# Two-layer transformer: four self-attention norms turned by TensorE instead of by DMAs, and the feed-forward norm of batch 0 earlier and in quarters

## The chip, the core and the metric

The kernel runs on one core of a Trainium2 chip. The metric is the device time of one execution in microseconds; several runs are taken and the median is given.

The engines, by the names of the profile: PE is TensorE (matmuls; PEld is its weight load, which overlaps), DVE is VectorE, ACT is ScalarE, POOL is GpSimd, SP is SyncE. SP does no arithmetic in this kernel: it is one in-order queue that issues nearly all DMAs after the start.

## The reference, cut to what matters

```
def _ln(x, g, b):
    m = mean(x); v = mean(square(x - m))
    return (x - m) * rsqrt(v + EPS) * g + b

def layer(x, context):                       # twice, with weights of its own
    h1 = _ln(x, n1_g, n1_b)
    x = _attn(h1, h1, q1, k1, v1, o1_w, o1_b, heads) + x
    h2 = _ln(x, n2_g, n2_b)
    x = _attn(h2, context, q2, k2, v2, o2_w, o2_b, heads) + x
    h3 = _ln(x, n3_g, n3_b)
    a, g = split(h3 @ ff_w1 + ff_b1, 2)
    return a * gelu(g) @ ff_w2 + ff_b2 + x
```

`_attn` is softmax attention with 20 heads of width 16. x is 4 batches x 512 tokens x 320, the context 4 x 1601 x 192, the hidden width of the feed-forward part 1280. All is 32-bit float. Each of the two layers has three norms per batch: 2 x 3 x 4 = 24 norms in the program.

## The kernel before, in words

**Units.** The order of all work is written out by a Python program that runs when the kernel is built. It goes through a list of units. An attention unit is one layer, self or cross, one batch b and one group g of four heads (5 groups). Self attention has 4 chunks of 128 keys per unit, cross attention 13. A feed-forward unit is one batch. Per layer come 20 self units, 20 cross units, 4 feed-forward units, so unit 37 is layer 0's cross attention, batch 3, group 2. The builder counts half chunks (`clock["round"]`): 8 per self unit, 26 per cross unit.

**A chunk** (`main`, L1270) issues for its unit the scores (L1280, matmul `st`, with the row maxima `nrows` as a third product), exponentials on ACT (L1290), and the products with the values (L1306, eight records per chunk, `av`), copied by ACT (L1325) and summed by POOL (L1326). In the same chunk it issues for the *next* unit the products of which only the row maxima are wanted: PE L1054 (`sps`), DVE L1069 (reductions to `nmax` or `pm`). At the end of a unit the maxima are laid out as rows (L1107 to L1131) and carried by DMA to `nrows`. The values' product comes once per chunk at a fixed place, so the distance between two of them is a chunk's length.

**Side work.** Everything else (norms, projections of queries, keys and values, the output's projection, the context's transposes) lies in queues, `chains`, entered by `add` (L428) with a cost in PE time, a due half chunk and two conditions. `steps` (L473) is called once or twice a chunk; it picks the due-first head whose conditions hold, and pays with a credit that `pace` fills. Steps with the cost LIGHT need no PE: at most `lights` of them are taken per call, which is 2 in a chunk without other products, 1 otherwise. At its end `steps` calls `carry` (L784), which puts DMAs on SP's queue: first the moves of finished queries and keys (L852), then errands, then the norms' bands, at most three per call.

**Side work by its names in the trace.** Projection of self attention's queries and keys: PE L886 (`qkps`), whose banks ACT empties into high and low halves (L897, L902, buffers `high` and `low`), which the moves (L852) carry to `q` and `kT`. Cross attention's queries: L927 (`qps`). Values: L1015 (`vps`). The context of a batch is turned into `ctxT`, stored by L741 and read back as the operand `w` by L755 (eight DMAs in two groups of four).

**A norm** (`add_norm`, L537) does for its batch, in this order:

- statistics of four token tiles of 128 tokens (DVE, L546 and L547), then the reciprocal root (L507 to L523: started on DVE, two Newton steps on POOL);
- then one of two forms, since the product needs features on partitions:
  - **the turned form** (`first` is true): three DVE scalings per token tile write the normalised tile in a permuted order to a buffer named `hturned` (`plain`, L608); TensorE turns it, four transposes per part and three parts (`turn`, L621, into a bank `hps`); ACT empties each part with gain and bias (L629) straight into `hT`;
  - **the DMA form**: per token tile one DVE normalisation to `hn` (L562) and one DVE transpose of 32 x 32 blocks into `hturned` (L568); then DMAs put the blocks into place in `hT` (`spread` and `move`, L578: 12 for a self or cross norm, 16 for a feed-forward norm); POOL applies gain and bias, three instructions (`affine`, L595);
- at last the next bias is added to x on POOL (`biased`, L601).

`due` is a norm's last date; its steps are due some fixed half chunks before. In the DMA form they are due `EARLIER` = 14 half chunks sooner than in the turned form, except feed-forward norms. `together` says how many token tiles one LIGHT step takes: two for a feed-forward norm, one otherwise. `landed` says how many half chunks `affine` waits after the last DMA of a part was issued: 4, and 2 for a feed-forward norm (`LANDS`). There is one `hturned` buffer; of `hT` there are two.

Before the change the turned form is used by self attention's norms of batches 0 and 1 in layer 0, and by cross attention's norm of batch 0 in both layers. The 20 others have the DMA form.

`add_norms` (L1372) enters the norms a few units ahead. A feed-forward norm gets `due` = its unit's start - 4.

Of the kernel before, what the change touches and what calls it, by code (L numbers as in the profile page):

```python
# [75 lines left out]
def kernel(ctx: ExitStack, tc: tile.TileContext, x, context, ws, out):  # L76
# [306 lines left out]
    clock = {"round": 0, "credit": 0.0, "lights": 0, "tiles": None, "ff": False}  # L383
# [142 lines left out]
    EARLIER = 14  # L526


    LANDS = (4, 2)
# [7 lines left out]
    def add_norm(l, b, i, put, done, due):  # L537
        xb = xs[b]
        s = {}
# [93 lines left out]
                hn_used.remove(b)  # L633
                put(s["hT"])

        first = i == 0 and b < 2 and l == 0 or i == 1 and b == 0
        ahead = 0 if first or i == 2 else EARLIER
        parts = [(0, 0, P, 0), (1, 4, 96, 0), (2, 7, 96, 0)]
        if i == 2:
            parts = [(0, 0, P, 0), (1, 4, P, 0), (2, 8, REST, 0), (2, 8, REST, REST)]  # L640
        left, moved = [len(parts) * P // SLOT], {}
# [2 lines left out]
            return lambda: clock["round"] >= s[key] + n  # L644

        def together(f):
            return [lambda ts=ts: [f(t) for t in ts] for ts in (((0, 1), (2, 3)) if i == 2 else ((0,), (1,), (2,), (3,)))]

        for t, f in enumerate(together(stats)):
            add(  # L650
                "norm", LIGHT, f, due - ahead - 22 + t,
                (lambda: stage[b] == 3 * l + i and not hn_used and b in loaded) if t == 0 else yes,
                (lambda: b == 0 or clock["round"] >= loaded[b] + 5) if t == 0 else yes,
            )
# [14 lines left out]
        for t, f in enumerate(together(lambda t: (normalise(t), blocks(t)))):  # L669
            add("norm", LIGHT, f, due - ahead - 13 + t, yes, yes if t else later(1))  # L670
# [3 lines left out]
            return lambda: k in moved and (k < 2 or not left[0])  # L674

        def landed(k):
            return lambda: clock["round"] >= moved[k] + LANDS[i == 2] and clock["round"] > s.get("scaled", 0)

        for k, n in enumerate((P, P, P) if i == 2 else (P, 96, 96)):
            add("scale", 0.0, lambda k=k, n=n: affine(k, n), due - 6 + k, there(k), landed(k))  # L680
# [87 lines left out]
    def lead(u):  # L768

        if u.i == 0:  # L770
            return 0
        return units[u.i - (AHEAD - 1 if u.early else 2 if u.m == 0 else 1)].start
# [595 lines left out]
    ff_read = []  # L1368
# [3 lines left out]
    def add_norms(i):  # L1372

        while norms and norms[0].i <= i + ((1 if norms[0].b else 3) if norms[0].kind == "ff" else AHEAD + 1 if norms[0].early else 8):
            u = norms.popleft()
            if u.kind == "ff":
                add_norm(u.l, u.b, 2, lambda t, u=u: setattr(u, "hT", t), lambda u=u: u in ff_read, u.start - 4)
            else:

                def done(u=u):  # L1380
                    return u.made["q"] == G and (u.cross or u.made["k"] == G and u.vmade[1] == u.nch)

                due = lead(u) - (10 if u.cross else 28)
                add_norm(u.l, u.b, int(u.cross), lambda t, u=u: u.own.update(h=t), done, due)
# [259 lines left out]
    now(load_x(1))  # L1644

    add_norms(0)
    add_proj(units[0])
    warm(5)
# [10 lines left out]
    first = units[0]  # L1659
# [24 lines left out]
    for i, u in enumerate(units):  # L1684
        nxt = units[i + 1] if i + 1 < len(units) else None
        before(u)
        if u.kind == "ff":

            flush()
            now(loads)  # L1690
            loads.clear()
            until_normed(lambda: u.hT is not None)
        clock["ff"] = u.kind == "ff"
        add_norms(i)
        for k in (3, SOON, AHEAD):
            v = units[i + k] if i + k < len(units) else None
            if v is not None and v.kind != "ff" and k == (SOON if not v.cross else AHEAD if v.early else 3):
                add_proj(v)
                if v.g == 0:
                    add_values(v)  # L1700
        (ff_main if u.kind == "ff" else main)(u, giver(u), nxt)
# [27 lines left out]
```

## Time and profile before

| | |
|---|---|
| median of 3 runs | 3010.82 us (3009.92 to 3014.1) |
| the profiled execution | 3011.88 us |
| its span | 3010.1 us, mean granted clock of TensorE 0.989 |
| PE busy | 2898.5 us (96%), 34970 matmuls |
| DVE busy | 2151.0 us (71%) |
| ACT busy | 1880.0 us (62%) |
| POOL busy | 1201.2 us (40%) |
| the norms' tiles, DMA form | DVE L562 and L568: 80 instructions each |
| the norms' tiles, turned form | DVE L608: 48, PE L621: 48 |
| the norms' transfers | SP L578: 272 |

How to read it: a line of the timeline has the start in us from the span's begin, the busy time, the engine, the line of the kernel, the operation and its tiles (out<-in), the shape and how many instructions stand in the row; in square brackets, where there is one, the idle time ahead of it and what ended that. A line of the windows has the stretch, its length, then the busy time of the engines with the number of instructions, then the granted clock of TensorE (1.00 is full speed), the share of the DMA engines, and GB/s. "SPq" is SP's queue, where a duration is that of issuing a DMA, its waits included.

### The profile page before, as it was taken

To read this page: it belongs to the slowest core of one execution; us is meant where nothing else is said; L and a number is where in the kernel's file an instruction comes from. 1 tells how busy PE (TensorE), PEld (TensorE's weight loads), DVE (VectorE), ACT (ScalarE), POOL (GpSimd) and SP (SyncE) were. 2 spreads that over 40 slices of the span, in tenths; PEclk is the share of its full clock that TensorE was granted. 3 is DMA by queue.
4 is the path that set the end of the run, shared out by engine and by line. 5 is a ranking of instruction groups with operands and counts; after the bars stand their busy time and mean duration, and the time that the engine had idled before them with its cause. 6 is when DMAs were issued, how large, how long until landed. Compare 5 with 4: busy or idle time off the path is not lost.

```text
span 3010.1 us, 84343 instructions
## 1 busy us (share of the span) xinstructions
PE 2898.5 (96%) x34970; PEld 1511.8 (50%) x34970; DVE 2151.0 (71%) x4138; ACT 1880.0 (62%) x3723; POOL 1201.2 (40%) x1317
## 2 busy tenths in 40 slices
PE   8989999999999999999999999999999999999999
PEld 4445555455555554355554555555555555544555
DVE  6777888889889888422258788888898888873221
ACT  3757677877877877611137676778778778774000
POOL 3445344544544543311114453445445454441110
PEclk8999999999999999999999999999999999999999
DMA  4444234223132122210114342221221121222000
GB/s 103 107 123 106 57 81 110 49 69 75 47 89 58 44 63 58 63 38 11 41 43 96 94 106 68 60 61 47 61 63 46 49 70 43 55 54 76 22 22 13
DMA packets 192430, 191.31 MB, mean 64 GB/s; under 512 B 70436, under 2 KB 143152, under 8 KB 192048
## 3 DMA queue, kind: packets, MB, share of 16 engines
q1 hardware_dynamic: 191256, 184.74, 24.3%
q8 instruction: 275, 4.51, 0.6%
q10 hardware_dynamic: 760, 1.18, 0.2%
q14 instruction: 107, 0.88, 0.1%
q0 software_dynamic: 32, 0.00, 0.0%
HBM read 55.76 MB, written 29.36 MB: 28 GB/s over the span
## 4 chain that ended last, share of the span: by engine, by line
PE 77%; DVE 17%; POOL 2%; issue 1%; DMA 1%; ACT 1%; SPq 1%; POOLq 0%; ACTq 0%; DVEq 0%
PE av L1306 21%; PE st L1280 15%; PE fps L1391 9%; DVE pm L1069 8%; PE sps L1054 6%; PE yps L1498 6%; PE vps L1015 5%; PE ops L1209 3%; PE kps L951 3%; DVE nmax L1069 3%; PE qkps L886 2%; PE fps L1451 2%; PE qps L927 2%; PE sps L1081 1%; DVE hn L562 1%
## 5 line engine op out<-in xcount | busy, mean ns | idle before, releaser
L1290 ACT ACTIVATE pr<-st 128x512 f32<-128x512 f32 (+1 forms) x2720 | 1405.3, 604 | 452.0 <-PE st L1280 405.4
L1069 DVE TENSOR_REDUCE pm<-sps 128x1 f32<-128x512 f32 x1920 | 1185.1, 680 | 134.1 <-PE sps L1054 124.8
L1326 POOL TENSOR_TENSOR o<-o,vo 128x512 f32<-128x512 f32 x576 | 739.9, 1284 | 1106.8 <-ACT vo L1325 1084.7
L1054 PE MATMUL sps<-kT,q 32*128 32x512 f32 x4800 | 880.8, 432 | 10.7 <-DMA q<-low 3.2
L1280 PE MATMUL st<-q,kT 32*128 32x512 f32 (+1 forms) x5120 | 799.3, 422 | 14.9 <-DVE pm L1069 10.7
L1306 PE MATMUL av<-pr,vals 128*32 128x512 f32 (+1 forms) x5440 | 741.1, 611 | 56.9 <-ACT pr L1290 16.0
L1280 PEld LDWEIGHTS st<-q,kT 32*128 32x128 f32 (+1 forms) x5120 | 423.6, 180 | 313.5 <-issue 118.6
L1280 PE MATMUL st<-nrows,ones 32*128 32x512 f32 (+1 forms) x2720 | 543.8, 400 | 7.6 <-DMA nrows<-turned 7.6
L1054 PEld LDWEIGHTS sps<-kT,q 32*128 32x128 f32 x4800 | 426.9, 185 | 104.8 <-DVE pm L1069 25.0
L1069 DVE TENSOR_REDUCE nmax<-sps 128x1 f32<-128x512 f32 x640 | 395.5, 679 | 75.7 <-PE sps L1054 69.9
L1325 ACT COPY vo<-av 128x512 f32<-128x512 f32 x576 | 353.7, 614 | 30.1 <-PE av L1306 27.9
L1462 ACT ACTIVATE gl<-fps,b 128x512 f32<-128x512 f32 x80 | 54.8, 687 | 414.3 <-PE fps L1451 303.0
L1391 PE MATMUL fps<-hT,w 128*128 128x512 f32 x640 | 283.0, 597 | 0.0
L1306 PEld LDWEIGHTS av<-pr,vals 128*32 128x32 f32 (+1 forms) x5440 | 111.0, 108 | 331.3 <-DVE pm L1069 182.7
L1280 PEld LDWEIGHTS st<-nrows,ones 32*128 32x128 f32 (+1 forms) x2720 | 247.3, 180 | 31.1 <-DMA nrows<-turned 7.5
L1463 DVE SCALAR_TENSOR_TENSOR hid<-fps,b,gl 128x512 f32<-128x512 f32 x80 | 59.7, 748 | 240.9 <-ACT gl L1462 238.8
L1391 PEld LDWEIGHTS fps<-hT,w 128*128 128x128 f32 x640 | 119.3, 190 | 155.3 <-issue 152.6
L1498 PE MATMUL yps<-w,hid 128*128 128x320 f32 x640 | 176.3, 435 | 0.1
L1498 PEld LDWEIGHTS yps<-w,hid 128*128 128x128 f32 x640 | 120.4, 190 | 56.5 <-ACT gl L1462 5.3
L1209 PEld LDWEIGHTS ops<-wo,aT 112*32 112x32 f32 (+1 forms) x3072 | 98.2, 111 | 62.7 <-issue 42.0
L1209 PE MATMUL ops<-wo,aT 112*32 112x160 f32 (+1 forms) x3072 | 125.9, 301 | 0.9 <-DVE pm L1069 0.8
L1505 DVE TENSOR_TENSOR x<-yps,x 128x320 f32<-128x320 f32 x32 | 15.7, 491 | 146.3 <-PE yps L1498 146.3
(89 smaller groups left out, 2465.1 us busy)
## 6 DMA issues: line engine op xcount, KB each, us to landing
kT<-stages SPq DMA_DIRECT2D x160, 200.2 KB
oway<-o SPq DMA_DIRECT2D x80, 256.0 KB
q<-high SPq DMA_DIRECT2D x160, 64.0 KB
q<-low SPq DMA_DIRECT2D x160, 64.0 KB
kT<-high SPq DMA_DIRECT2D x60, 128.0 KB
q<-high SPq DMA_DIRECT2D x60, 128.0 KB
kT<-low SPq DMA_DIRECT2D x57, 128.0 KB
hT<-hturned SPq DMA_DIRECT2D x112, 64.0 KB
```

What stands on the lines that cost most here:

```text
L951: nc.tensor.matmul(ps[(i * GT + f) * SLOT : (i * GT + f + 1) * SLOT, :w], lhsT=wk2[:, k, u.g * GD + f * SLOT : u.g * GD + (f + 1) * SLOT], ...
L1015: nc.tensor.matmul(ps[f : f + m, :w], lhsT=u.kvT[:n, k, at + f : at + f + m], rhs=wv[:n, k, h0 * DH : h1 * DH], start=(k == 0), stop=(k == ...
L1054: nc.tensor.matmul(ps, lhsT=u.q[j * SLOT : (j + 1) * SLOT, e, t * P : (t + 1) * P], rhs=u.kT[j * SLOT : (j + 1) * SLOT, u.k0 + s * 512 : u ...
L1069: nc.vector.tensor_reduce(to[:, j : j + 1], ps, AX.X, ALU.max, negate=(ns == 1))
L1209: nc.tensor.matmul(ps[f : f + m, : D // 2], lhsT=aT[:n, k, f * NQ + t * SLOT : f * NQ + t * SLOT + m], rhs=wo[:n, k, cols], start=(k == 0) ...
L1280: nc.tensor.matmul(own[0][:r, :], lhsT=ones[rows, :r] if e == 2 else u.keys(rows, c), rhs=u.rows[rows, :] if e == 2 else u.q[rows, e, :], ...
L1290: nc.scalar.activation(p[:r], own[0][:r], AF.Exp)
L1306: nc.tensor.matmul(ps[j * SLOT : (j + 1) * SLOT, :], lhsT=columns_of[:r, head : head + SLOT], rhs=pr.pop((c, j))[:r, :], start=True, stop= ...
L1325: nc.scalar.copy(vo, ps)
L1326: nc.gpsimd.tensor_tensor(u.o, u.o, vo, ALU.add)
L1391: nc.tensor.matmul(ps, lhsT=w1[:, k, i * FF + c * P : i * FF + (c + 1) * P], rhs=natural(u.hT[:, k]), start=start, stop=stop,)
L1498: nc.tensor.matmul(ps[:, :D], lhsT=hid[c][:, t * P : (t + 1) * P], rhs=w2[:, c, :], start=(c == 0), stop=(c == NHC - 1),)
```

## The change

```diff
-        first = i == 0 and b < 2 and l == 0 or i == 1 and b == 0
-        ahead = 0 if first or i == 2 else EARLIER
+        first = i == 0 and (l == 0 or b > 1) or i == 1 and b == 0
+        ahead = 0 if first or i == 2 and b else EARLIER
...
         def together(f):
-            return [lambda ts=ts: [f(t) for t in ts] for ts in (((0, 1), (2, 3)) if i == 2 else ((0,), (1,), (2,), (3,)))]
+            return [lambda ts=ts: [f(t) for t in ts] for ts in (((0, 1), (2, 3)) if i == 2 and b else ((0,), (1,), (2,), (3,)))]
...
         def landed(k):
-            return lambda: clock["round"] >= moved[k] + LANDS[i == 2] and clock["round"] > s.get("scaled", 0)
+            return lambda: clock["round"] >= moved[k] + LANDS[i == 2 and b > 0] and clock["round"] > s.get("scaled", 0)
...
-                add_norm(u.l, u.b, 2, lambda t, u=u: setattr(u, "hT", t), lambda u=u: u in ff_read, u.start - 4)
+                add_norm(u.l, u.b, 2, lambda t, u=u: setattr(u, "hT", t), lambda u=u: u in ff_read, u.start - (4 if u.b else 40))
```

i is 0 for self attention's norm, 1 for cross attention's, 2 for the feed-forward part's.

1. `first`: the self norms of batches 2 and 3, in both layers, change from the DMA form to the turned form. Layer 1's batches 0 and 1 keep the DMA form. Over the program PE's transposes (L621) go from 48 to 96, ACT's evictions of them (L629) from 11 to 23, DVE's scalings (L608) from 48 to 96; DVE's normalisations and block transposes (L562, L568) from 80 to 64 each, POOL's affines (L595) from 60 to 48, SP's transfers (L578) from 272 to 224.
2. `ahead` and the due time: the feed-forward norm of batch 0 is due 36 half chunks sooner, and its statistics, root and tiles 14 more.
3. `together`: that norm takes one token tile per LIGHT step, not two.
4. `landed`: that norm waits 4 half chunks after the last DMA of a part, not 2.

The other feed-forward norms are as before.

## The prediction

> **What bounds the kernel now.** I read the page first: its span, the engines' shares, the chain that ended last by engine.
>
> ```profile
> span 3010.1 us, 84343 instructions
> PE 77%; DVE 17%; POOL 2%; issue 1%; DMA 1%; ACT 1%; SPq 1%; POOLq 0%; ACTq 0%; DVEq 0%
> ```
>
> The profiled run took 3011.88 us, 1.8 outside its span; the median of the three runs is 3010.82, so 1.06 lower. PE (TensorE) carries the chain, DVE (VectorE) the next part of it. Time is won where PE waits, or where its order gets shorter. So I went through PE's timeline at the places that the diff touches, and measured stretches between the starts of the values' products (L1306), which come once per key chunk. What a stretch takes above its own matmuls is its **excess**.
>
> **The feed-forward norm of batch 0.** The first rows are PE's in layer 0, around unit 37 to 38 (cross attention, batch 3); then DVE's in the same stretch, and its windows with PE busy, PE's weight loads, DVE, ACT and POOL busy, the granted clock, the DMA share and GB/s.
>
> ```profile
> 1180.76 1.06 PE L1306 MATMUL av<-pr,vals 128*32 128x512 f32 x8 [0.22 <-ACT pr L1290]
> ...
> 1195.80 1.32 PE L1280 MATMUL st<-q,kT 32*128 32x512 f32 x4 [2.42 <-DVE pm L1069]
> ...
> 1204.51 1.07 PE L1306 MATMUL av<-pr,vals 128*32 128x512 f32 x8
> ...
> 1209.77 1.06 PE L1306 MATMUL av<-pr,vals 128*32 128x512 f32 x8
> ```
>
> ```profile
> 1190.14 1.39 DVE L562 TENSOR_SCALAR hn<-x,mv,root 128x320 f32<-128x320 f32 x1 [0.42 <-POOL root L523]
> ...
> 1195.09 4.84 DVE L1069 TENSOR_REDUCE pm<-sps 128x1 f32<-128x512 f32 x8
> ```
>
> ```profile
> 1195.00:1201.00 6.00, 5.11 (x34) 2.17 (x38) 5.14 (x10) 1.67 (x3) 0.68 (x1) 0.72 0.57 157
> ```
>
> Two undisturbed chunks, 1204.51 to 1209.77, take 5.26 us, so one takes 2.63. The six chunks from 1180.76 to 1204.51 take 23.75 where 6 x 2.63 = 15.78 would do: 7.97 excess. The cause stands on DVE: from 1190.14 to 1195.09 it does nothing but four normalised tiles and their four block transposes, 4.95 us in one piece. Behind them the pair maxima (L1069) are late, PE waits 2.42 for them, and the granted clock falls to 0.72 over the next six microseconds, which is the larger part of the excess. [...]
>
> **Self attention's norms.** Layer 0, batch 3: PE's rows, then SP's queue, then the same two chunks' work in a quieter place.
>
> ```profile
> 205.72 1.07 PE L1306 MATMUL av<-pr,vals 128*32 128x512 f32 x8
> ...
> 216.08 1.15 PE L1054 MATMUL sps<-kT 32*128 32x512 f32 x2 [5.58 <-ACT low L902]
> ...
> 224.44 1.07 PE L1306 MATMUL av<-pr,vals 128*32 128x512 f32 x8
> ```
>
> ```profile
> 197.81 0.58 SPq L741 DMA_DIRECT2D ctxT<-stages  x1
> ...
> 203.68 2.89 SPq L755 DMA_DIRECT2D w<-ctxT  x4
> ...
> 213.05 0.60 SPq L852 DMA_DIRECT2D q<-low  x1
> ```
>
> ```profile
> 1702.86 1.07 PE L1306 MATMUL av<-pr,vals 128*32 128x512 f32 x8
> ...
> 1712.97 1.07 PE L1306 MATMUL av<-pr,vals 128*32 128x512 f32 x8
> ```
>
> 18.72 against 10.11: 8.6 excess. PE's 5.58 us wait is for the projection's bank, held until ACT can write the low halves of the queries; their buffer is freed by a move (L852) that stood on SP, one in-order queue, behind the context's loads (L755, which wait for the stores L741) and the norm's own transfers.
>
> Layer 1, batch 3, DVE's rows, PE's rows and a clean twin; then batch 2 of layer 0 and of layer 1.
>
> ```profile
> 1682.35 1.36 DVE L562 TENSOR_SCALAR hn<-x,mv,root 128x320 f32<-128x320 f32 x1 [3.86 <-POOL root L523]
> ...
> 1684.29 0.45 DVE L562 TENSOR_SCALAR hn<-x,mv,root 128x320 f32<-128x320 f32 x1
> ...
> 1684.77 0.51 DVE L568 STREAM_TRANSPOSE hturned<-hn 128x320 f32<-128x320 f32 x1
> ```
>
> ```profile
> 1680.33 1.06 PE L1306 MATMUL av<-pr,vals 128*32 128x512 f32 x8 [0.21 <-ACT pr L1290]
> ...
> 1694.52 1.06 PE L1306 MATMUL av<-pr,vals 128*32 128x512 f32 x8
> ```
>
> ```profile
> 1621.16 1.06 PE L1306 MATMUL av<-pr,vals 128*32 128x512 f32 x8
> ...
> 1628.79 1.06 PE L1306 MATMUL av<-pr,vals 128*32 128x512 f32 x8
> ```
>
> ```profile
> 103.51 1.07 PE L1306 MATMUL av<-pr,vals 128*32 128x512 f32 x8 [0.21 <-ACT pr L1290]
> ...
> 114.91 1.06 PE L1306 MATMUL av<-pr,vals 128*32 128x512 f32 x8
> ```
>
> ```profile
> 1604.25 1.07 PE L1306 MATMUL av<-pr,vals 128*32 128x512 f32 x8 [0.21 <-ACT pr L1290]
> ...
> 1615.85 1.06 PE L1306 MATMUL av<-pr,vals 128*32 128x512 f32 x8
> ```
>
> 14.19 - 7.63 = 6.6 excess; DVE stood 3.86 us waiting for the root's last step, which POOL reached late; the later tiles take 0.45 and 0.51 each. Batch 2: 11.40 - 7.63 = 3.8 and 11.60 - 7.63 = 4.0. The four self norms that change form stand in 8.6 + 6.6 + 3.8 + 4.0 = 23.0 us of excess. That is a ceiling, not a gain: the root stays, and the context's loads stay.
>
> **The change part by part. Edits 2 to 4, the feed-forward norm.** Due times move 50 half chunks up for its statistics, root and tiles; as built, the four tiles go out two in one chunk and two in the next, about 18 half chunks before their old place, where all four fell in one chunk. Nothing is added: the same 4 tiles, 16 transfers, 4 affines on POOL; the transfers enter SP's queue earlier, when the stage is in the same steady state. What does it cost two tiles per chunk? The cross norm of batch 1 runs so in the same kind of stage. PE's first and last row, then the windows' row for the values' pieces (L1015) alone and for the queries' piece (L927) alone.
>
> ```profile
> 499.50 1.07 PE L1306 MATMUL av<-pr,vals 128*32 128x512 f32 x8 [0.28 <-ACT pr L1290]
> ...
> 519.32 1.07 PE L1306 MATMUL av<-pr,vals 128*32 128x512 f32 x8
> ```
>
> ```profile
> 499.50:519.30 19.80, 3.16 (x64) 2.04 (x64) 1.00 0.52 141
> ```
>
> ```profile
> 499.50:519.30 19.80, 1.48 (x24) 0.78 (x24) 1.00 0.52 141
> ```
>
> 19.82 us hold five chunks, 13.15, and 3.16 + 1.48 = 4.64 of pieces: 2.0 excess, and 3.2 if a quarter of the pieces' time overlaps the chunks' own; the clock stayed at 1.00. I take 3.2, the dearer, because the two pairs stand in neighbouring chunks. The row maxima of the next unit end near the old place, so I leave one late reduction there; the page's group gives its mean, 679 ns:
>
> ```profile
> L1069 DVE TENSOR_REDUCE nmax<-sps 128x1 f32<-128x512 f32 x640 | 395.5, 679 | 75.7 <-PE sps L1054 69.9
> ```
>
> Gain per layer 7.97 - 0.7 - 3.2 = 4.1, two layers **8.2**. Bounds: 2 x (7.97 - 0.7 - 2.0) = 10.5 at best; at worst the stall moves whole, 0. The longer wait after the last transfer (4 half chunks for 2) and the longer hold of the tile cost nothing while the affines stand tens of half chunks ahead of the first reader; if batch 0's tile came late, the feed-forward stage's first matmul would show it.
>
> **Edit 1, four self norms.** Removed per norm: 12 transfers on SP (0.6 us of issue each, as the L852 row), 3 POOL affines, 4 normalise and 4 block-transpose instructions of DVE. Added: 12 DVE scalings, 12 PE transposes, 3 ACT evictions. What goes from POOL and SP is worth only what it frees there, and that is counted in the excess above. The transposes lie on PE, so on the path; the scalings and evictions lie beside other work on DVE and ACT, and what of them shows is inside the price that I take from the cross norm of batch 0, which has this form already:
>
> ```profile
> 242.75 1.06 PE L1306 MATMUL av<-pr,vals 128*32 128x512 f32 x8
> ...
> 247.87 1.06 PE L1306 MATMUL av<-pr,vals 128*32 128x512 f32 x8
> ...
> 250.59 1.06 PE L1306 MATMUL av<-pr,vals 128*32 128x512 f32 x8
> ...
> 262.86 1.53 PE L621 MATMUL hps<-ident,hturned 128*128 128x128 f32 x12 [0.74 <-DVE nmax L1069]
> ...
> 266.60 1.06 PE L1306 MATMUL av<-pr,vals 128*32 128x512 f32 x8
> ```
>
> ```profile
> 262.00:268.00 6.00, 5.14 (x64) 3.31 (x64) 5.73 (x10) 5.18 (x10) 4.57 (x5) 1.00 0.62 142
> ```
>
> The raw matmuls take 1.53. The three chunks around them take 16.01; one of them holds a double projection (such a chunk takes 247.87 - 242.75 = 5.12), the others 2.63 each, with two values' pieces like this one:
>
> ```profile
> 500.38 0.83 PE L1015 MATMUL vps<-wv,w 96*32 96x192 f32 x16
> ```
>
> That is 5.12 + 2 x 2.63 + 2 x 0.83 = 12.0, or 11.5 if a third of the pieces overlaps. So the norm costs 4.0 to 4.5 there, with a wait for DVE in it, in six microseconds with DVE busy 5.73 and ACT 5.18. Bounds 1.5 to 4.5, I take the middle, 3.0; four norms **12.0** (6.1 to 18). [...]
>
> What is left of the 23.0: layer 1's b=3 root is still on POOL behind the same products, and its 3.86 us wait stays in most part (I take 3); with the transposes directly behind each other, b=3's projection follows the last one without a chunk between, 0.6 per layer; in layer 0 the row maxima's transfers now stand behind the context's loads, where the queries' moves stood, 1. Together 5. Net: 23.0 - 12.0 - 5.2 = **5.8**. Bounds: at worst nothing of the excess goes and each transpose costs 4.5, -18; at best all goes at the raw price, +16.9.
>
> Sum: 8.2 + 5.8 = 14.0; 3011.88 - 14.0 = 2997.9 for such an execution, and 1.06 lower for the median: **2996.8, say 2997**. Its own range, by self net 0 to 12 and feed-forward 5 to 10.5: 2988 to 3006.
>
> **The rivals.**
>
> *Only the feed-forward part pays.* Self's stalls shrink by just what the transposes cost: 3010.82 - 8.2 = 3002.6. For it: the waits named are SP's context loads and POOL's root, which the change doesn't touch. Against: the 12 transfers and 3 affines per norm go from just these two queues.
>
> *All of it goes, at the raw price.* 16.9 + 10.5 = 27.4: 2983.4. For it: the clock at 0.72 doubles what a wait costs, so a wait avoided pays twice. Against: the one turned norm in a full stage cost 4.0 to 4.5.
>
> *Slower: the waits outlive the transfers.* If PE's stalls belong to L755's wait and to POOL's order, all 23.0 stay, and the turned norms add 18: 3010.82 + 18 - 8.2 = 3020.6. It decides as soon as less of the 23.0 goes than the transposes cost beyond 8.2: under 9.8 at the price of 4.5, under 3.8 at 3.0. For it: L755's four loads still enter SP's queue at almost the same chunk. Against: as built, the moves of layer 0's b=3 queries come after all of those loads and not between them.
>
> *The sooner turn only moves its stall.* Two neighbouring chunks with two tiles each are 3.9 us of DVE (2 x 2 x (0.45 + 0.51) by batch 1's form); in a stage in which DVE is near its limit that is one stall for another, gain 0, and with self net 0 the time stays: 3010.8. With self at its 5.8 it would be 3005.
>
> **How the numbers follow.** Forecast 0.45, only feed-forward 0.18, all goes 0.12, waits outlive 0.13, stall only moves 0.12. A measurement here can tell some 0.2%, 6 us, from no change: under 3004.8 is faster, over 3016.8 slower. Faster: 0.44 + 0.14 + 0.12 = 0.70. Same: the rest of the first two, 0.05, and 0.10 of the last. Slower: 0.13 and 0.02 of the last. Range: 2984 to 3014 leaves out half of "all goes" (0.06) and nearly all of "waits outlive" (0.12).
>
> **What would show it.** Feed-forward: no DVE stretch of four tiles ahead of an L1069 row in the chunks of the old place, no 2.4 us wait there, the granted clock near 1; in the new place at most 3 us more per layer. Self: the wait on ACT's low halves in layer 0's b=3 gone; L621 twelve more times four; the chunks around them at 1.5 to 4.5 above their pieces. Wrong: the same waits at the same chunks with transposes beside them, a new PE wait for hturned or for the row maxima, a granted clock below 0.9 around L621, or the first L1391 waiting for the affine.

## The result and the profile after

The changed kernel takes 3002.41 us (median of 8 runs, 2996.16 to 3006.56) against 3011.15 for the kernel before (8 runs): ratio 0.997, 95% interval 0.996 to 0.9981. That is 8.7 us faster, 5.7 to 12.0 by the interval. The forecast was 2997, 14.0 faster in a like execution, in a range of 2984 to 3014.

The page of the changed kernel: its span, the chain by engine, and the group of the values' products with its idle time and what ended it.

```profile
span 2999.1 us, 84363 instructions
...
PE 77%; DVE 18%; DMA 1%; issue 1%; ACT 1%; POOL 1%; SPq 1%; ACTq 0%; DVEq 0%; POOLq 0%
...
L1306 PE MATMUL av<-pr,vals 128*32 128x512 f32 (+1 forms) x5440 | 738.4, 609 | 74.7 <-DVE nmax L1069 19.3
```

The chain shows nothing: its shares are the same within a per cent. The last row does. The values' products now stand idle 19.3 us for the row maxima on DVE, where the view of PE's waits has 2.5 in the kernel before. A new wait has come in.

To see where, I number the values' products (680 in both kernels, one per key chunk) and lay the two timelines side by side. Here are the same eight products, number 0, 50, 300, 310, 320, 400, 635 and 660, in the kernel before:

```profile
54.84 1.06 PE L1306 MATMUL av<-pr,vals 128*32 128x512 f32 x8
...
277.04 1.07 PE L1306 MATMUL av<-pr,vals 128*32 128x512 f32 x8
...
1142.95 1.06 PE L1306 MATMUL av<-pr,vals 65*32 65x512 f32 x8
...
1176.65 1.06 PE L1306 MATMUL av<-pr,vals 128*32 128x512 f32 x8
...
1212.29 1.06 PE L1306 MATMUL av<-pr,vals 128*32 128x512 f32 x8
...
1805.16 1.06 PE L1306 MATMUL av<-pr,vals 128*32 128x512 f32 x8
...
2605.91 1.06 PE L1306 MATMUL av<-pr,vals 128*32 128x512 f32 x8
...
2693.67 1.07 PE L1306 MATMUL av<-pr,vals 128*32 128x512 f32 x8
```

and in the changed kernel:

```profile
51.10 1.07 PE L1306 MATMUL av<-pr,vals 128*32 128x512 f32 x8
...
263.77 1.07 PE L1306 MATMUL av<-pr,vals 128*32 128x512 f32 x8
...
1128.40 1.07 PE L1306 MATMUL av<-pr,vals 65*32 65x512 f32 x8
...
1166.95 1.06 PE L1306 MATMUL av<-pr,vals 128*32 128x512 f32 x8
...
1194.95 1.06 PE L1306 MATMUL av<-pr,vals 128*32 128x512 f32 x8
...
1795.65 1.06 PE L1306 MATMUL av<-pr,vals 128*32 128x512 f32 x8
...
2596.31 1.06 PE L1306 MATMUL av<-pr,vals 128*32 128x512 f32 x8
...
2682.83 1.07 PE L1306 MATMUL av<-pr,vals 128*32 128x512 f32 x8
```

Subtracting each stretch from its twin:

| stretch | before | after | difference |
|---|---|---|---|
| up to product 0 (nothing changed there) | 54.84 | 51.10 | -3.7, chance (below) |
| 0 to 50: layer 0's self norms of b=2 and 3 | 222.20 | 212.67 | **-9.5** |
| 50 to 300: nothing changed there | 865.91 | 864.63 | -1.3 |
| 300 to 310: the feed-forward norm's new place | 33.70 | 38.55 | +4.9 |
| 310 to 320: its old place | 35.64 | 28.00 | -7.6 |
| 320 to 400: layer 1's self norms of b=2 and 3 | 592.87 | 600.70 | **+7.8** |
| 400 to 635: nothing changed there | 800.75 | 800.66 | -0.1 |
| 635 to 660: the feed-forward norm of layer 1, both places | 87.76 | 86.52 | -1.2 |

So the gain is a remainder. Layer 0's self norms gave 9.5, layer 1's took 7.8 back, and the feed-forward norms gave 2.8 and 1.2. That is 5.7 in this one pair of traces, where the medians say 8.7 (5.7 to 12.0). The 3.7 ahead of product 0 are no part of it: over six kernels that are the same up to there, product 0 starts between 50.97 and 54.84. How far one such stretch can be trusted: where the order of the instructions is the same in both kernels, single chunks still differ by 1.0 to 1.7 us between two executions, a few times in 2700 us. One of them, 1.7, stands in the last row: with edits 2 to 4 alone that stretch was 84.74 (its rows come below), 3.0 less than before.

### The profile page after: what moved, and what is told of

Read it like the earlier page. It is cut to its first block, busy times and chain, and to the rows that moved or that the text cites. A ratio compares the mean times of both kernels' runs of the same rounds, so it can differ in the third digit from the quotient of the medians.

```text
span 2999.1 us, 84363 instructions
## 1 busy us (share of the span) xinstructions
PE 2885.4 (96%) x35018; PEld 1509.7 (50%) x35018; DVE 2150.8 (72%) x4143; ACT 1892.7 (63%) x3746; POOL 1194.0 (40%) x1305
## 4 chain that ended last, share of the span: by engine, by line
PE 77%; DVE 18%; DMA 1%; issue 1%; ACT 1%; POOL 1%; SPq 1%; ACTq 0%; DVEq 0%; POOLq 0%
PE av L1306 21%; PE st L1280 15%; PE fps L1391 9%; DVE pm L1069 9%; PE sps L1054 6%; PE yps L1498 6%; PE vps L1015 4%; DVE nmax L1069 4%; PE ops L1209 3%; PE kps L951 3%; PE qkps L886 3%; PE fps L1451 2%; PE qps L927 2%; PE sps L1081 1%; DVE hturned L608 1%
## 5 line engine op out<-in xcount | busy, mean ns | idle before, releaser
L1306 PE MATMUL av<-pr,vals 128*32 128x512 f32 (+1 forms) x5440 | 738.4, 609 | 74.7 <-DVE nmax L1069 19.3
L1209 PEld LDWEIGHTS ops<-wo,aT 112*32 112x32 f32 (+1 forms) x3072 | 98.0, 110 | 64.6 <-issue 42.9
```

The source lines that it names most:

```text
L1209: nc.tensor.matmul(ps[f : f + m, : D // 2], lhsT=aT[:n, k, f * NQ + t * SLOT : f * NQ + t * SLOT + m], rhs=wo[:n, k, cols], start=(k == 0) ...
L1306: nc.tensor.matmul(ps[j * SLOT : (j + 1) * SLOT, :], lhsT=columns_of[:r, head : head + SLOT], rhs=pr.pop((c, j))[:r, :], start=True, stop= ...
```

## The experiments

All ratios are against the kernel before, on the same chip, five rounds; its medians were 3010.76, 3011.25 and 3011.43 in the three groups of four. The three groups ran on different chips, so a difference between groups, or from the changed kernel's 3002.41, can be off by some tenths of a us. Theory A was each time the account that the traces so far spoke for, and rival B the prediction's or the nearest other.

### Which edit pays, and in which layer

```diff
ff_only: edits 2 to 4
-        first = i == 0 and (l == 0 or b > 1) or i == 1 and b == 0
+        first = i == 0 and b < 2 and l == 0 or i == 1 and b == 0
self_only: edit 1, the rest as before
layer0_and_ff:
+        first = i == 0 and l == 0 or i == 1 and b == 0
```

> Edits 2 to 4 alone, all self norms as before. Theory A, from laying the two traces chunk by chunk: the feed-forward edits give 2.8 us in layer 0 and 1.2 in layer 1, 4 in all (the four tiles cost 5 to 6 in their new place and the 7.7 of the old place goes): about 3007. Rival B, the sizes of the prediction: 8.2: about 3003.

> Edit 1 alone, all four self norms turned, the feed-forward norm as before. Theory A: layer 0 gives about 9.5 us and layer 1 takes about 7.8 back, so 1.7 faster, 3009. Rival B: both layers give alike, 5.8 in all: 3005.

> The changed kernel, but layer 1's batches 2 and 3 keep the DMA form. Theory A: 7.8 us faster than the changed kernel, about 2995, and 16 under before. Rival B: half of self's gain is gone, so 2.9 slower than the changed kernel, about 3005.

| kernel | median, us | against before | ratio, 95% interval |
|---|---|---|---|
| edits 2 to 4 alone | 3003.86 | -6.9 | 0.9975, 0.9965 to 0.9985 |
| edit 1 alone | 3005.30 | -5.5 | 0.9981, 0.9972 to 0.9989 |
| all, but layer 1's self norms as before | 2993.57 | **-17.2** | 0.9938, 0.9926 to 0.9951 |
| all (the changed kernel) | 3002.41 | -8.7 | 0.997, 0.996 to 0.9981 |

The third run decides: without layer 1's two turned norms the kernel is 8.8 us faster than with them, as A said (7.8), and not 2.9 slower. By the medians layer 0's two norms give 3003.86 - 2993.57 = 10.3. The two halves alone lie between the theories, both nearer to B's 3003 and 3005 than to A's 3007 and 3009, and add up to 12.4 rather than 8.7; the intervals are 3 us to each side, so that is not told apart from noise. The trace of edit 1 alone has layer 0's 9.7 and layer 1's loss of 7.8 as in the table, so 1.9, and doesn't show where the median's 5.5 comes from. In the trace of edits 2 to 4 alone, products 635 and 660:

```profile
2597.63 1.07 PE L1306 MATMUL av<-pr,vals 128*32 128x512 f32 x8
...
2682.37 1.07 PE L1306 MATMUL av<-pr,vals 128*32 128x512 f32 x8
```

84.74 against 87.76 of before: 3.0 in layer 1, as the 2.8 in layer 0.

### Place or quarters

```diff
ff_sooner_pairs: edits 2 and 4 alone
+            return [... for ts in (((0, 1), (2, 3)) if i == 2 else ((0,), (1,), (2,), (3,)))]
layer0_ff_one_tile: layer0_and_ff, and batch 0's tiles one per chunk
-            add("norm", LIGHT, f, due - ahead - 13 + t, yes, yes if t else later(1))
+            add("norm", LIGHT, f, due - ahead - 13 + t, yes,
+                (later(2) if i == 2 and not b else yes) if t else later(1))
```

> Edits 2 and 4 alone: batch 0's feed-forward norm sooner, but still two token tiles per LIGHT step, so four in one chunk; self norms as before. Theory A1: what pays is the place (longer chunks with more room on DVE), so within 1.5 us of edits 2 to 4. Rival A2: what pays is the split; then the stall of before only moves and the time is that of before, 3011.

> The changed kernel with layer 1's batches 2 and 3 in the DMA form, and batch 0's feed-forward norm one tile per chunk rather than two. Theory A: the norm's price in its new place, 4.9 us per layer, is DVE's two tiles being more than the room of a chunk; spread over four chunks it falls to 2 or 3, so about 4 us under 2993.6, 2989.5. Rival B: even one tile is more than the room, or the statistics ahead are most of the price: within 1.5 us of 2993.6.

In pairs it took 3009.55, ratio 0.9995 (0.9986 to 1.0004): the stall only moved. Products 300 and 310 of that kernel, the new place:

```profile
1140.91 1.06 PE L1306 MATMUL av<-pr,vals 65*32 65x512 f32 x8
...
1183.08 1.06 PE L1306 MATMUL av<-pr,vals 128*32 128x512 f32 x8
```

42.17 against 33.70: 8.5 us is the price of the norm with four tiles in one piece, and its old place gives back 7.7. With two tiles per chunk, in the changed kernel, it was 4.9. One per chunk took 2991.08 (0.993, 0.9916 to 0.9943), 2.5 under the kernel that it was made from (`layer0_and_ff`; the intervals overlap). Products 300 and 310:

```profile
1129.83 1.07 PE L1309 MATMUL av<-pr,vals 65*32 65x512 f32 x8
...
1167.10 1.06 PE L1309 MATMUL av<-pr,vals 128*32 128x512 f32 x8
```

37.27: 3.6, and 83.57 from product 635 to 660 in layer 1. The traces of the two kernels differ by 1.3 and 1.2 there, together the 2.5 of the medians. So A2 holds for the pairs and theory A for the single tiles, with 2.5 of the 4 expected. What pays is how few tiles stand together on DVE; standing earlier alone pays nothing, and the split in the old place wasn't tried. What is left of the price was not taken apart. DVE's rows in the changed kernel show how little room a chunk has: two tiles are 2.3 to 2.5 us, and the maxima behind them run late over two chunks, in one piece.

```profile
1149.86 0.98 DVE L562 TENSOR_SCALAR hn<-x,mv,root 128x320 f32<-128x320 f32 x1
1150.88 0.51 DVE L568 STREAM_TRANSPOSE hturned<-hn 128x320 f32<-128x320 f32 x1
...
1152.34 4.84 DVE L1069 TENSOR_REDUCE pm<-sps 128x1 f32<-128x512 f32 x8
```

### What layer 0's self norms gained from

Products 36 and 38 of the changed kernel, in layer 0's batch 3, where the 5.58 us wait on ACT's low halves was:

```profile
196.92 1.07 PE L1306 MATMUL av<-pr,vals 128*32 128x512 f32 x8
...
206.71 1.06 PE L1306 MATMUL av<-pr,vals 128*32 128x512 f32 x8
```

9.79 us where before took 18.72. Is it the twelve transfers that are gone from SP's queue, or the context's loads, which stand elsewhere? In the changed kernel those loads start at 181.34 and 187.28 us, three products sooner than before, ahead of the queries' moves (probably since the norm's LIGHT steps are due later and leave the context's their turn). The experiment keeps every norm in its old form and moves the loads alone:

```diff
load_later: the kernel before
             dma(out=saved[b][:, :, c0 * 32 : (c0 + n) * 32], in_=s[i][:, :, : n * 32])
+            saved_at[b] = clock["round"]
...
-            add("context", 0.0, lambda k=k: load(k), due - 14 + 2 * k, free if k == 0 else yes, later(2) if k else yes)
+            add("context", 0.0, lambda k=k: load(k), due - 14 + 2 * k, free if k == 0 else yes, later(2) if k else lambda: clock["round"] >= saved_at[b] + 6)
```

> The kernel before, all norms in its form, but the context's first group of loads is issued at least six half chunks after its last store (in layer 0's batch 3 of self attention at half chunk 78 rather than 72, so behind the moves of the queries). Theory A: the 5.58 us wait of PE there belongs to those loads, which stand on SP waiting for the stores; it goes without any turning, and the two chunks of 11.88 and 6.84 us fall to about 6.0 and 4.7: 5 to 8 us faster than before, about 3004. Rival B: it belongs to the norm's twelve transfers in the same queue; then those two chunks keep over 16 us together and the time stays at 3011.

Products 36 and 38 of it, and SP's row of the second group of loads, now behind the moves:

```profile
207.68 1.06 PE L1309 MATMUL av<-pr,vals 128*32 128x512 f32 x8
...
217.79 1.06 PE L1309 MATMUL av<-pr,vals 128*32 128x512 f32 x8
```

```profile
219.64 3.23 SPq L758 DMA_DIRECT2D w<-ctxT  x4
```

10.11 us: the wait is gone with all twelve transfers of the norm in place. So it belonged to the loads. The time did not follow, though: 3011.31, ratio 0.9997 (0.9988 to 1.0006). In the trace 4.7 us come back between products 52 and 56 (22.57 against 17.85), where PE waits 1.51 for ACT's low halves, and 4.4 between 104 and 106, where it waits 2.72 for the maxima's rows. That these are the price of moving the loads is not shown: the delayed loads stand at products 37 and 38, and `root_later` below takes as long between 104 and 106 without the delay. In the profile 5.0 more stand between products 28 and 33, where the order of the instructions is unchanged; that I can't explain by the edit. The profiled execution took 3016.74, the longest of this kernel's eleven, so it may show losses that the median has not. A is right on the cause of the wait and wrong on the gain from removing it.

### What layer 1's self norms pay

In layer 1's batch 3 of the changed kernel: POOL's last step of the root and its next sum, DVE's six scalings behind it, PE's product behind the maxima, and the window after (columns as in the prediction).

```profile
1667.19 0.20 POOL L523 TENSOR_TENSOR root<-root,root 128x4 f32<-128x4 f32 x1
1667.34 1.26 POOL L1326 TENSOR_TENSOR o<-o,vo 128x512 f32<-128x512 f32 x1
```

```profile
1667.43 2.67 DVE L608 TENSOR_SCALAR hturned<-x,mv,root 128x128 f32<-128x128 f32 x6 [2.38 <-POOL root L523]
...
1669.99 2.47 DVE L1069 TENSOR_REDUCE nmax<-sps 128x1 f32<-128x512 f32 x4
```

```profile
1670.72 1.94 PE L1306 MATMUL av<-pr,vals 128*32 128x512 f32 x8 [4.25 <-DVE nmax L1069]
```

```profile
1667.00:1675.00 8.00, 4.28 (x32) 1.38 (x32) 5.50 (x13) 1.67 (x4) 1.52 (x3) 0.63 0.38 108
```

DVE still waits for the root, 2.38 us in place of 3.86. Behind it the turned form puts 2.67 us of scalings in one piece. The DMA form put no less there: in the kernel before, its first two tiles fill the time from 1682.35 to 1685.21, the first of them 1.36 us long. Its first block transpose, and the maxima behind the two tiles:

```profile
1683.74 0.51 DVE L568 STREAM_TRANSPOSE hturned<-hn 128x320 f32<-128x320 f32 x1
...
1685.21 2.45 DVE L1069 TENSOR_REDUCE nmax<-sps 128x1 f32<-128x512 f32 x4
```

So the stall has not gone, it stands one chunk sooner: PE waits 4.25 for the maxima, the granted clock is 0.63 from 1667 to 1675, and products 371 to 376 take 26.77 us where they took 25.83. The rest of the 7.8 is spread: 1.2 between products 350 and 355, where batch 2's stall was, 1.6 between 355 and 371, and 3.5 between 378 and 390, which also take over side work that stood sooner before.

Laid beside layer 0, the same forty chunks (products 10 to 50 and 350 to 390) took 180.04 and 167.27 us before and take 170.47 and 174.14 now. The two layers are nearer to each other in the turned form than in the DMA form. Of the 12.8 that layer 0 was behind, 8.6 is the pair of chunks with the 5.58 us wait; in layer 1 the same pair took 10.11 from the start (the prediction's twin), so that there was nothing to win.

Five runs take the price apart: the transposes doubled, the scalings made cheaper in two ways, and the root given more time in two kernels.

```diff
turned_twice: every transpose issued twice into the same place
             for t in range(NQ):
+                for _ in range(2):
                     nc.tensor.transpose(ps[:n, t * P : (t + 1) * P], s["hn"][:, t * D + at : t * D + at + n], ident)
plain_one: one scaling per tile, in plain order (the permutation is left out)
+            nc.vector.tensor_scalar(s["hn"][:, t * D : (t + 1) * D], xb[:, t, :], s["mv"][:, t, 0:1], s["rstd"][:, t : t + 1], ALU.subtract, ALU.mult)
two_scalings: two per tile
+            for at, n, h in ((0, P, 1), (P, 192, 2)):
root_later, all norms; layer0_ff_root, self norms only, layer 1 in the DMA form
-            add("norm", LIGHT, ..., yes, yes if t else later(1))
+            add("norm", LIGHT, ..., yes, yes if t else later(3))
```

> The changed kernel with every transpose of the turned norms issued twice into the same place (96 more, 12 for each of eight norms). Theory A: TensorE's own part of a turned norm is its raw 1.53 us, of which some lies in room that PE has while DVE is behind: 0.8 to 1.5 each, 6 to 12 us slower than the changed kernel, 3008 to 3014, and the clock granted around them stays at 1.0. Rival B: TensorE's part is most of the 4.0 to 4.5 measured before for one norm: over 25 us slower.

> The changed kernel, but each token tile of a turned norm is scaled by one DVE instruction into plain order instead of three into the permuted order (so the features come out in another order: the permutation is left out). 64 DVE instructions fewer, some 0.75 us less per tile. Theory A: in layer 1, where the turned form cost time, it is DVE's scalings that cost, 2.46 us in a piece ahead of the maxima: 3 to 5 us come back there, and 5 to 9 in all, about 2995. Rival B: the price is PE's and ACT's; under 2 us come back.

> The changed kernel with the turned form's scalings in two DVE instructions per token tile rather than three (the two blocks of 96 features in one). Theory A: on DVE each instruction of 96 to 320 features takes about the same 0.4 us, so 0.4 per tile goes, half of what one instruction per tile took away; that gave 12 us, so this gives about 6: 2996.5. Rival B: the joined instruction takes as long as the two, and nothing is won: 3002.5.

> The changed kernel, but every norm's first tile waits three half chunks after the second Newton step rather than one. Theory A: in layer 1's batch 3 DVE stands 2.38 us on POOL's root and PE 4.25 on the maxima behind it; with the wait longer that chunk of 7.35 us falls to 4 or less, and the whole is 3 to 5 us faster than the changed kernel, about 2998.5. Rival B: the tiles fall into chunks with as little room on DVE, and nothing is won: 3002.

> The changed kernel with layer 1's batches 2 and 3 in the DMA form, and self attention's norms start their first tile three half chunks after the root's last step rather than one. Theory A: in layer 1's batch 3 DVE's wait of 3.84 us for POOL goes, and with it 3 to 5 us: about 2989.5. Rival B: the tiles meet chunks with as little room and the time stays at 2993.6.

**The transposes are cheap.** With all 96 doubled it took 3008.48 (0.9992, 0.9983 to 1.0001), 6.1 over the changed kernel: 0.8 us for each of eight norms. Where a norm's 24 stand, and the window around:

```profile
263.42 2.84 PE L622 MATMUL hps<-ident,hturned 128*128 128x128 f32 x24
```

```profile
252.00:276.00 24.00, 20.90 (x264) 11.07 (x257) 19.90 (x40) 18.05 (x35) 10.45 (x11) 1.00 0.42 109
```

The raw matmuls grew by 2.84 - 1.53 = 1.31, of which 0.8 shows in the mean of the eight, and the clock stays at 1.00 over these 24 us, with the transposes standing between other matmuls.

**The scalings are dear.** One scaling per tile took 2990.3 (0.9927, 0.9915 to 0.994), 12.1 under the changed kernel, 1.5 us per norm. Its features come out in another order, so it is a measure of the price and not a kernel to use. The order of writing changes too, but it is hardly what counts: scalings that no POOL instruction overlaps take 0.40 to 0.41 us on average for 96 to 192 features in the permuted order, and 0.44 for 320 in the plain one. In the trace 3.9 of it come from layer 0 (product 0 to 50) and 7.7 from layer 1 (320 to 400), which is about what layer 1 had lost. Of the 7.7, 4.4 stand in products 371 to 376 (22.41 us): PE still waits 3.31 for the maxima there, but the granted clock is 1.00 over the stretch, where the changed kernel has 0.87. DVE's group of it:

```profile
L606 DVE TENSOR_SCALAR hturned<-x,mv,root 128x320 f32<-128x320 f32 x32 | 19.9, 667 | 3.5 <-POOL root L523 3.4
```

and the two groups of the changed kernel, then of the kernel with two scalings:

```profile
L608 DVE TENSOR_SCALAR hturned<-x,mv,root 128x96 f32<-128x96 f32 x64 | 21.6, 394 | 0.0
L608 DVE TENSOR_SCALAR hturned<-x,mv,root 128x128 f32<-128x128 f32 x32 | 21.3, 665 | 3.5 <-POOL root L523 3.4
```

```profile
L608 DVE TENSOR_SCALAR hturned<-x,mv,root 128x192 f32<-128x192 f32 x32 | 20.9, 654 | 0.0
L608 DVE TENSOR_SCALAR hturned<-x,mv,root 128x128 f32<-128x128 f32 x32 | 20.9, 652 | 3.5 <-POOL root L523 3.5
```

The total falls from 42.9 to 19.9 us with one scaling, but only to 41.8 with two, and the time to 3000.24 (0.9964, 0.9951 to 0.9976), 2.2 where A said 6. B was nearer: the joined instruction takes 654 ns in the mean, though the median over this kernel's scalings is 410. The last section says why.

**The root's wait goes and comes back.** With three half chunks between root and tiles the changed kernel took 2998.3 (0.9948, 0.9934 to 0.9961), 4.1 better, and the chunk behind product 371 fell from 7.35 us to 3.18. In its trace products 340 to 400 take 5.9 less (252.99 for 258.94), but products 338 to 340, with layer 0's feed-forward stage between them, 5.5 more (307.55 for 302.04), so the trace as a whole doesn't show the 4.1. And where layer 1 keeps the DMA form the same edit took 2993.13 (0.9937, 0.9925 to 0.995) against 2993.57, nothing. Products 372 and 373 without the longer wait, then 372 to 375 with it:

```profile
1666.23 1.06 PE L1306 MATMUL av<-pr,vals 128*32 128x512 f32 x8 [0.20 <-ACT pr L1290]
...
1674.59 1.93 PE L1306 MATMUL av<-pr,vals 128*32 128x512 f32 x8
```

```profile
1663.54 1.06 PE L1306 MATMUL av<-pr,vals 128*32 128x512 f32 x8
...
1668.05 1.06 PE L1306 MATMUL av<-pr,vals 128*32 128x512 f32 x8
...
1672.25 1.06 PE L1306 MATMUL av<-pr,vals 128*32 128x512 f32 x8
...
1678.92 1.93 PE L1306 MATMUL av<-pr,vals 128*32 128x512 f32 x8
```

The chunk of 8.36 falls to 4.51, and two chunks on one of 3.37 becomes 6.67, where the next two tiles now stand. B again: the chunks there have no room on DVE.

### All together

`all_mends` is layer 1 in the DMA form with two scalings, one feed-forward tile per chunk and the longer wait in self attention.

> Layer 1's batches 2 and 3 in the DMA form, with all three: two scalings per tile, one feed-forward tile per chunk, the root's wait longer in self attention. Theory A: they add up, 4 + 4 + about 3 (the six turned norms that are left): about 2982.5. Rival B: they share the same room on DVE and give no more than the best of them, about 2989.

It took 2990.68 (0.9937, 0.9924 to 0.9949). Rival B: no more than the best of its parts, `layer0_ff_one_tile` with 2991.08. That one is 20 us faster than the kernel before and 11 faster than the changed one.

## Why the prediction was right or wrong

- **Direction and range** held, the size did not: 8.7 where 14.0 was forecast, and the interval ends at 12.0.
- **The excess at the feed-forward norm's old place**, 7.97, was right as a size: 7.6 came back. But the prediction calls the slowed clock its larger part, and by its own row the clock at 0.72 over 6.00 us costs 1.7 (an estimate, 0.28 x 6.00), less than the wait of 2.42, which it does not double either, as the rival "all of it goes" has it. The other 3.9 are neither.
- **Edits 2 to 4**, 8.2 forecast. By the medians 6.9, by the trace 2.8 + 3.0 = 5.8. The old place gave back 7.6, near the 7.3 taken. The term that was mis-sized is the price in the new place, 3.2 by the row of batch 1's cross norm, 4.9 measured; why it is dearer here was not taken apart. The rival "the sooner turn only moves its stall" comes true only in the kernel without quarters, 3009.55 (its 3.9 us of DVE are 3.84).
- **Edit 1**, 5.8 forecast, 5.5 measured alone, and still wrong, so that the near size is luck: on top of the other edits it is +10.3 in layer 0 less 8.8 in layer 1. The step that failed is the one sum of 23.0 us of excess over both layers, with 5 left. In layer 0 more went than the 12.4 that I had found there: 8.9 between products 36 and 38 and 5.2 between 10 and 32, with 4.5 added between 38 and 50. In layer 1 none of the 10.6 went (25.83 to 26.77 and 20.23 to 21.41 at its two places), and the norms' own price came on top. The prediction's sign of being wrong, "a new PE wait for hturned or for the row maxima", came: 19.3 us for 2.5, 13.3 of them in layer 1.
- **"Layer 1's root wait stays in most part, 3"** was right as a wait (2.38 for 3.86) and too low as a price: behind it DVE has as much in one piece as before, 2.67 us for 2.86, so the maxima are as late (PE waits 4.25 for them), and a slowed clock comes with them again, 0.63 from 1667 to 1675.
- **The price of a turned norm**, 3.0: the experiments give 0.8 for PE and 1.5 for DVE's scalings beyond one per tile, 2.3 in the mean over eight norms. The scalings' part is uneven: 7.7 of the 12.1 stand in products 320 to 400, with three of the eight. ACT's evictions were not priced alone. The step "the transposes lie on PE, so on the path; the scalings and evictions lie beside other work" has it the wrong way round. In the norms' chunks PE had room, because it waits for DVE (4.25 us in layer 1's batch 3); DVE had none ahead of the maxima, which stand there behind 2.67 us of scalings.
- **Layer 0's batch 3**: "the wait on ACT's low halves gone" came true, 18.72 to 9.79. The reason given, the loads and the norm's transfers together, was half right: the loads alone do it.
- The rival "the waits outlive the transfers" came true in layer 1 only.
- **Open**: why the two halves of the change give 12.4 alone and 8.7 together, if it is not noise; the 5.0 us before the loads in that one profile; and which of layer 1's two batches could still be turned with gain, which wasn't tried.

## What to carry to other kernels

Where two engines are both near their limit, price a rewrite by what it puts on each in one piece, not by the engine that leads the chain: here eight DVE scalings cost about twice what twelve transposes cost, 1.5 us for 0.8. A sum of excess over several places is a ceiling for each place alone; find out for each what ends its wait before adding. And lay two timelines side by side by a product that comes once per step: a change of 8.7 us was one of 17 with a loss of 9 inside.

## What the runs showed of the hardware

A short DVE instruction can last until a POOL instruction beside it ends, 1.13 us where it takes 0.17 elsewhere; I call it held. In the changed kernel, DVE's step of the root in layer 1's batch 3, and POOL's at the same time:

```profile
1659.14 1.13 DVE L511 TENSOR_SCALAR root<-root 128x4 int32<-128x4 int32 x1
```

```profile
1658.96 1.29 POOL L804 TENSOR_TENSOR low<-low,high 128x512 f32<-128x512 f32 x1
```

The same DVE instruction took 0.17 at nineteen of the 24 norms; here it ends at 1660.27, with POOL's at 1660.25. The other four long ones, 1.13 to 1.17, also began while POOL was at work and ended within 0.03 us of it. The prediction's first tile of 1.36 us at 1682.35 is of the same kind: it ended at 1683.71, and POOL's sum ran from 1682.26 to 1683.52.

Not every DVE instruction that meets POOL is held. Two scalings of 96 features and the one of 128 behind them, in layer 0 of the changed kernel, and POOL's sum at the same time:

```profile
107.89 0.68 DVE L608 TENSOR_SCALAR hturned<-x,mv,root 128x96 f32<-128x96 f32 x2
...
108.46 1.10 DVE L608 TENSOR_SCALAR hturned<-x,mv,root 128x128 f32<-128x128 f32 x1
```

```profile
108.14 1.28 POOL L1326 TENSOR_TENSOR o<-o,vo 128x512 f32<-128x512 f32 x1 [7.27 <-ACT vo L1325]
```

The two of 96 are done while POOL runs; the one of 128 ends 0.14 behind POOL. So it is in all 96 scalings of this kernel: 13 of the 32 scalings of 128 began with 0.3 us or more of a POOL instruction to go, and all 13 ended 0.14 us behind it, after 0.75 to 1.36; the others took about 0.40. Of the 64 scalings of 96 none took more than 0.42, though 22 met POOL in the same way. That is what lies between 394 and 665 ns in the scalings' groups above, and why joining two of them saved almost nothing: of the 32 joined ones of 192, 10 were held, up to 1.47 us. The join made of a pair that POOL doesn't hold one that it does. Why the 96 go free, by their width or by their three blocks of 32 where 128 has four, no run here tells.

By what means POOL's instruction holds DVE's is not shown, and no run changes POOL's work alone.
